# Two bottleneck blocks on one core: a relu moved to ScalarE, the products reordered at the ends of streams, and wider statistics products

## The chip, the cores and the metric

The kernel runs on one core of one Trainium2 chip. The metric is the device time of one execution in microseconds (us). The median of three executions before the change is 1967.26 us, with the others at 1964.27 and 1967.46 us.

The engines are called as the profile calls them: PE is TensorE (matmuls), PEld its weight loads, DVE is VectorE, ACT is ScalarE, POOL is GpSimd, SP is SyncE, which here only issues transfers. A "q" behind an engine's name means its queue: the part that waits and issues transfers.

## The reference

The program computes two bottleneck blocks of a residual network, one after the other, in float32, on 64 images of 1024 channels and 14 x 14 pixels. Cut to what matters, one block is:

```python
out = relu(bn(conv(x, w1, b1)))          # 1x1, 1024 -> 256 channels
out = relu(bn(conv(out, w2, b2, pad=1))) # 3x3,  256 -> 256
out = bn(conv(out, w3, b3))              # 1x1,  256 -> 1024
out = softplus(residual_scale)[0] * out
return relu(x + out)
```

`bn` takes the mean and variance of each channel over all 64 images, so each convolution must be complete (or its statistics known) before its result is normalised. Block 1 has its own weights and takes block 0's output as `x`.

## The kernel before, in words

**Stages.** The 64 images are cut into 32 tiles (T) of two images (PX = 392 pixels). In order of time: the first 1x1 convolution of block 0 (0 to 300 us), the 3x3 convolution of block 0 (300 to 600), its Gram matrix and the statistics of the third convolution (600 to 690), a fused stage that does the last convolution of block 0 and the first of block 1 side by side (690 to 1280), the 3x3 convolution of block 1 (1280 to 1565), its Gram matrix and statistics (1565 to 1660), and the last stage, which does the third convolution of block 1, the residual sum and the final relu (1660 to the end). Block 0's output goes through DRAM (`mid`) and is loaded again in the last stage.

**Seven products for eight.** The 1x1 convolutions are done by a scheme with seven block products instead of eight. Class `Seven` (L253) names them `p1` to `p7`, and each is followed by what takes it out of PSUM (`after1` to `after7`). Three banks are used by a unit: `y` takes p1, and then p6, p7 and p4 are added to it; `x` takes p2; `p` takes p5, and then p3 is added to it. Between the additions, ScalarE copies the bank out (`saved`: u1 after p1, u2 after p6, u3 after p7), because the next product adds to the same bank. So p6 waits for u1, p7 for u2, p4 for u3, and p3 waits until VectorE has added what p5 left in `p` to the residual (`after5`, `add`, L458).

**The stream.** `stream` (L299) puts units one behind the other, so that each unit's last two products, p3 and p4, stand after the next unit's p1. A unit in the middle gives PE the order p1, p3 and p4 of the unit before, p6, p2, p5, p7. All matmuls keep the program's order. `beside` runs a piece of other work between products in the first stage. There are four streams: the first stage, the two of the fused stage, and the last stage.

**The last stage.** `final` (L1134) walks over pairs of tiles. A pair has four units (q = 0 to 3); each `Conv3Pair` (L495) makes channel slots q and q + 4 (rows 0 and 1) of both tiles (i = 0, 1). Its seven products are one matmul of 392 columns each, which the profile shows as two records. Around them stand, for each unit: four adds from PSUM to the residual on VectorE (L458, after2, after5, after3, after4), three copies on ScalarE (L325, `cu`), three adds on GpSimd (L479 for u3, L505 twice for u1 and u2), and four relus with the shift. Row 0's two relus are on ScalarE in `end` (L507), row 1's two on VectorE in `go_out` (L512, the operation at L516), which then sends both rows of both tiles out (L520). Once per pair, `column_sums` (L415, operations at L422 to L425) makes the inputs t1 to t4 of the next pair's products on VectorE. `go_out` of a unit is called when the generator of units is resumed, as are the loads of two further tiles (L123, `x<-mid`, five buffers), which wait until the tiles that lay in their buffers have gone out. SP issues loads and outputs in one order.

**The statistics of the third convolution.** `conv3_stats` (L1076) gets mean and mean square of each output channel from the Gram matrix. It makes `by_mean`, the weights times the mean of their input channel, with two scaled copies on ScalarE (L1092) and an add on GpSimd (L1093); `q`, the weights times a product with the Gram matrix, on VectorE (L1104, L1105); and sums both over the partitions by matmuls whose moving operand is a single column of ones: eight for `by_mean` and eight for `q`, all into one bank `ax`. One copy (L1110) brings them to SBUF, `affine` (L1215) makes scale and shift out of them, and `residual` (L1115) then begins to add the first tile's products, some of which (`made`) PE has done meanwhile.

**The start.** `busy` (L170) gives PE products that nothing uses, of the identity with one of its columns, while the first data are on their way.

## Time and profile before

| what | value |
| --- | --- |
| median of three executions | 1967.26 us |
| profiled execution, its span | 1971.1 us |
| PE busy | 1932.2 us (98%) |
| DVE busy | 1578.6 us (80%) |
| ACT busy | 1022.2 us (52%) |
| POOL busy | 545.0 us (28%) |
| moved between DRAM and SBUF | 408.39 MB, mean 207 GB/s |
| mean granted TensorE clock | 0.994 of full speed |

The span is what one execution took under the profiler. Busy shares are means over stages with different limits, so they don't tell what an edit is worth; the view of windows (busy time of each engine in a given stretch of the span) and the timeline (single instructions with the idle time before them and what ended it) do. The end of a matmul in a trace is modelled; where a number here rests on matmuls, it is taken from their starts.

### The profile page before, as it was taken

Reading aid. Unit: us, or ns where it says so; the run is one execution under the profiler, and the core shown is the slowest. Engines: PE = TensorE matmul, PEld = TensorE weight load, DVE = VectorE, ACT = ScalarE, POOL = GpSimd, SP = SyncE. Lnnn points to the kernel's source line nnn. Section 1 sums busy time; section 2 is a strip of 40 time slices with the busy share of each in tenths; the row PEclk is TensorE's granted clock in tenths of the full one; section 3 lists DMA queues with packets and bytes.
Section 4 is the critical chain, followed back from the end, with each engine's and each line's share of the span. In section 5 each row is a group of like instructions: output and inputs, shape, how many; then the busy total and the mean of one; then the engine's idle time right before and its main releaser. Section 6 shows DMA issues by size and latency. Waiting matters only on the chain.

```text
span 1971.1 us, 27055 instructions
## 1 busy us (share of the span) xinstructions
PE 1932.2 (98%) x9428; PEld 1617.8 (82%) x9428; DVE 1578.6 (80%) x2544; ACT 1022.2 (52%) x2026; POOL 545.0 (28%) x640
## 2 busy tenths in 40 slices
PE   9999999999999999999999999989999999999998
PEld 5555557999998799999999999989999886555555
DVE  5778768999997667677776776699999975889997
ACT  2222214676765155555555555457677632555555
POOL 0111100100105133433433433200010051666665
PEclk9999999999999999999999999999999999999999
DMA  7776725676748534444444444257676395799998
GB/s 289 276 249 247 259 99 167 176 209 196 199 135 211 187 132 187 172 164 180 180 164 176 182 167 168 95 183 210 197 197 200 117 213 217 262 325 334 339 330 296
DMA packets 188983, 408.39 MB, mean 207 GB/s; under 512 B 24944, under 2 KB 165136, under 8 KB 172336
## 3 DMA queue, kind: packets, MB, share of 16 engines
q1 hardware_dynamic: 161728, 324.66, 48.3%
q0 software_dynamic: 21504, 30.94, 6.9%
q10 hardware_dynamic: 5616, 51.06, 6.2%
q8 instruction: 75, 1.23, 0.3%
q14 instruction: 60, 0.49, 0.1%
HBM read 263.75 MB, written 115.34 MB: 192 GB/s over the span
## 4 chain that ended last, share of the span: by engine, by line
PE 85%; DVE 7%; DMA 5%; issue 1%; ACT 1%; SPq 0%; POOL 0%; DVEq 0%; ACTq 0%
PE ay L168 17%; PE cy L168 13%; PE columns L168 13%; PE cp L168 11%; PE ap L168 10%; PE m L168 6%; PE l L168 6%; PE ax L168 5%; PE cx L168 4%; DMA x<-mid 3%; DVE x L458 1%; DMA out<-x 1%; PE ps L168 1%; DVE x L516 1%; DMA home<-y 1%
## 5 line engine op out<-in xcount | busy, mean ns | idle before, releaser
L325 ACT ACTIVATE cu<-cy,scale 128x196 f32<-128x196 f32 (+1 forms) x552 | 256.8, 474 | 299.5 <-PE cy L168 292.2
L168 PE MATMUL columns<-v,ub 128*128 128x224 f32 (+1 forms) x1536 | 303.4, 339 | 0.7 <-ACT columns L755 0.7
L168 PEld LDWEIGHTS columns<-v,ub 128*128 128x128 f32 x1536 | 271.3, 190 | 4.5 <-ACT columns L755 1.2
L325 ACT ACTIVATE x<-x,shift 128x392 f32<-128x392 f32 x368 | 211.5, 614 | 68.6 <-POOL x L484 53.1
L458 DVE SCALAR_TENSOR_TENSOR x<-cp,scale,x 128x196 f32<-128x196 f32 (+1 forms) x368 | 178.0, 484 | 84.8 <-PE cp L168 81.3
L168 PE MATMUL cy<-ct,ws 128*128 128x196 f32 (+1 forms) x736 | 221.8, 383 | 2.5 <-ACT cu L325 2.5
L479 POOL TENSOR_TENSOR x<-x,cu 128x196 f32<-128x196 f32 (+1 forms) x184 | 167.3, 909 | 171.5 <-ACT cu L325 170.8
L168 PE MATMUL ay<-at,ws 128*128 128x196 f32 (+1 forms) x752 | 209.3, 381 | 1.0 <-ACT au L325 1.0
L484 POOL TENSOR_TENSOR x<-x,cu 128x392 f32<-128x392 f32 x124 | 125.9, 1015 | 191.1 <-DVE x L458 181.4
L168 PEld LDWEIGHTS ay<-at,ws 128*128 128x128 f32 x752 | 136.3, 190 | 35.1 <-ACT au L325 1.9
L168 PEld LDWEIGHTS cy<-ct,ws 128*128 128x128 f32 x736 | 133.6, 190 | 36.9 <-ACT cu L325 3.8
L168 PE MATMUL m<-sums,ua 128*128 128x224 f32 (+1 forms) x752 | 147.1, 339 | 6.2 <-DVE sums L619 6.2
L168 PE MATMUL l<-diffs,ub 128*128 128x224 f32 (+1 forms) x768 | 149.7, 338 | 2.5 <-PE columns L168 2.5
L505 POOL TENSOR_TENSOR x<-x,cu 128x392 f32<-128x392 f32 x120 | 125.0, 1042 | 84.2 <-DVE x L458 74.6
L866 POOL DMA_DIRECT2D y<-f x24 | 31.1, 1533 | 414.2 <-DVE f L796 414.2
L168 PEld LDWEIGHTS l<-diffs,ub 128*128 128x128 f32 x768 | 133.8, 189 | 6.6 <-PE columns L168 5.1
L168 PEld LDWEIGHTS m<-sums,ua 128*128 128x128 f32 x752 | 131.6, 190 | 8.4 <-DVE sums L619 8.0
L325 ACT ACTIVATE au<-ay 128x196 f32<-128x196 f32 (+1 forms) x141 | 53.6, 380 | 156.8 <-PE ay L168 156.2
L458 DVE SCALAR_TENSOR_TENSOR x<-cx,scale,x 128x196 f32<-128x196 f32 (+1 forms) x184 | 89.1, 484 | 52.1 <-PE cx L168 51.5
L168 PE MATMUL cx<-y,w 128*128 128x196 f32 (+1 forms) x404 | 126.4, 399 | 0.0
L168 PE MATMUL cy<-y,w 128*128 128x196 f32 (+1 forms) x404 | 125.3, 396 | 0.0
L168 PE MATMUL cp<-zt 128*128 128x257 f32 x392 | 118.9, 385 | 2.0 <-DVE zt L1025 1.7
(209 smaller groups left out, 3997.4 us busy)
## 6 DMA issues: line engine op xcount, KB each, us to landing
x<-in_x SPq DMA_DIRECT2D x62, 1568.0 KB, 6.7
ub<-u SPq DMA_DIRECT2D x94, 768.0 KB, 5.2
x<-mid SPq DMA_DIRECT2D x32, 1568.0 KB, 9.1
mid<-x ACTq DMA_DIRECT2D x31, 1568.0 KB, 5.1
out<-x SPq DMA_DIRECT2D x123, 392.0 KB, 7.0
ua<-u SPq DMA_DIRECT2D x94, 256.0 KB, 3.0
u<-y POOLq DMA_DIRECT2D x48, 256.0 KB, 6.3
home<-y SPq DMA_DIRECT2D x90, 96.0 KB, 4.8
```

What stands on the lines that cost most here:

```text
L168: tc.keep_in_program_order(nc.tensor.matmul(*args, **kw))
L325: tc.keep_in_program_order(nc.scalar.activation(*args, **kw))
L458: nc.vector.scalar_tensor_tensor(v, bank, self.scale[:, o : o + 1], v, ALU.mult, ALU.add)
L479: nc.gpsimd.tensor_add(self.part(1, 1), self.part(1, 1), u3)
L484: nc.gpsimd.tensor_add(v, v, self.u12)
L505: nc.gpsimd.tensor_add(v, v, self.u12[:, i * self.n : (i + 1) * self.n])
L516: nc.vector.tensor_scalar(v, v, self.shift[:, o : o + 1], 0.0, ALU.add, ALU.max)
L866: nc.gpsimd.dma_start(out=out_rows[0][:, o], in_=f[:, o], accum_op=ALU.add)
```

## The change

There are five edits.

1. In `Conv3Pair`, one of row 1's two relus (i = 1) moves from VectorE (`go_out`) to ScalarE (`end`, first of three).
2. `stream` looks one unit ahead. The first unit of a stream does p2 before p6, and the last unit does p2 after p7 instead of before p5, so that a product stands where PE would have waited for a ScalarE copy. To know which unit is the last, the generator is now resumed before a unit's products are issued, where it was resumed after them. What the generator does on being resumed (in the last stage `go_out`, the loads and `column_sums`) is thereby called one unit earlier.
3. In `conv3_stats` the sums over the partitions stream 64 equal columns of ones instead of one, into two banks (`ax`, `ap`) with a copy from each.
4. There too, `by_mean` is made by two VectorE operations instead of two on ScalarE and one on GpSimd.
5. The products at the start use a tile of ones that VectorE sets, instead of the identity, and there are three instead of two.

```diff
     def stream(items, beside=lambda: None):
-        before = None
-        for now in items:
+        before, items = None, iter(items)
+        now = next(items)
+        while now is not None:
+            following = next(items, None)
             yield from now.p1()
             if before is not None:
                 beside()
                 yield from before.last()
                 beside()
+            else:
+                yield from now.p2()
             yield from now.p6()
             if before is not None:
                 before.end()
-            beside()
-            yield from now.p2()
+                if following is not None:
+                    beside()
+                    yield from now.p2()
             beside()
             yield from now.p5()
             beside()
             yield from now.p7()
             beside()
-            before = now
+            if following is None:
+                yield from now.p2()
+            before, now = now, following
         yield from before.last()
         before.end()
...
         def end(self):
-            for i in range(2):
-                o, v = self.o[0], self.part(0, i)
+            for row, i in (1, 1), (0, 0), (0, 1):
+                o, v = self.o[row], self.part(row, i)
                 act(v, v, AF.Relu, bias=self.shift[:, o : o + 1])

         def go_out(self):
-            for i in range(2):
-                o, v = self.o[1], self.part(1, i)
-                tc.keep_in_program_order(
-                    nc.vector.tensor_scalar(v, v, self.shift[:, o : o + 1], 0.0, ALU.add, ALU.max)
-                )
+            o, v = self.o[1], self.part(1, 0)
+            tc.keep_in_program_order(nc.vector.tensor_scalar(v, v, self.shift[:, o : o + 1], 0.0, ALU.add, ALU.max))
...
-        quad = psum.tile(2 * CS, "ax").rearrange("p (o k) -> p o k", k=2)
+        wide = 64
+        sums = [psum.tile(CS * wide, tag).rearrange("p (o k) -> p o k", k=wide) for tag in ("ax", "ap")]
...
-        by_mean, more = (spare[:, s * C : (s + 1) * C] for s in range(MS))
-        for s, to in enumerate((by_mean, more)):
-            nc.scalar.activation(to, w3[:, s].rearrange("p o c -> p (o c)"), AF.Identity, scale=means[s])
-        nc.gpsimd.tensor_add(by_mean, by_mean, more)
+        ones = ones[:, :1].to_broadcast([P, wide])
+        by_mean, w = spare[:, :C], [w3[:, s].rearrange("p o c -> p (o c)") for s in range(MS)]
+        nc.vector.tensor_scalar(by_mean, w[0], means[0], None, ALU.mult)
+        nc.vector.scalar_tensor_tensor(by_mean, w[1], means[1], by_mean, ALU.mult, ALU.add)
...
         for o in range(CS):
-            matmul(quad[:, o, 0:1], by_mean[:, o * P : (o + 1) * P], ones, start=True, stop=True)
+            matmul(sums[0][:, o], by_mean[:, o * P : (o + 1) * P], ones, start=True, stop=True)
         for o in range(CS):
-            matmul(quad[:, o, 1:2], q[:, 0, o * P : (o + 1) * P], ones, start=True, stop=True)
-        nc.vector.tensor_copy(mv, quad)
+            matmul(sums[1][:, o], q[:, 0, o * P : (o + 1) * P], ones, start=True, stop=True)
+        nc.vector.tensor_copy(mv[:, :, 0], sums[0][:, :, 0])
+        nc.vector.tensor_copy(mv[:, :, 1], sums[1][:, :, 0])
...
+    ones = y_all[:, 0, NPX // 2 : NPX // 2 + P]
+    nc.vector.memset(ones, 1.0)
...
-        busy(psum, "ay", 2)
+        busy(psum, "ay", 3, ones)
```

More of the change, by code (lines that the diff above doesn't have):

```diff
@@ L168, in matmul, with busy @@
         tc.keep_in_program_order(nc.tensor.matmul(*args, **kw))
-    def busy(psum, tag, n):
+    def busy(psum, tag, n, with_=None):
+        v = ident if with_ is None else with_
         for i in range(n):
-            matmul(psum.tile(448, tag), ident, ident[:, :1].to_broadcast([P, 448]), start=True, stop=True)
+            matmul(psum.tile(448, tag), v, v[:, :1].to_broadcast([P, 448]), start=True, stop=True)
     def filters(pieces, spare):
```

## The prediction

> **What bounds the kernel now.** I read the page first: busy time and the chain that ended last.

> ```profile
> PE 1932.2 (98%) x9428; PEld 1617.8 (82%) x9428; DVE 1578.6 (80%) x2544; ACT 1022.2 (52%) x2026; POOL 545.0 (28%) x640
> ...
> PE 85%; DVE 7%; DMA 5%; issue 1%; ACT 1%; SPq 0%; POOL 0%; DVEq 0%; ACTq 0%
> ```

> PE is busy nearly throughout and carries 85% of the chain. So a gain can only come from PE's idle pieces and from stretches in which PE is busy but slow. I looked for the slow stretches in the view of windows, cut at the two statistics stages (columns after the colon: length, busy time of PE, PEld, DVE, ACT and POOL, then the granted clock).

> ```profile
> 672.79:676.21 3.42, 3.42 (x25) 2.72 (x23) 2.66 (x4) 0.00 (x0) 0.12 (x1) 1.00 0.00 0
> 676.21:679.62 3.41, 3.41 (x14) 3.02 (x14) 1.03 (x6) 0.10 (x1) 0.00 (x0) 0.50 0.88 283
> 679.62:683.03 3.41, 3.41 (x6) 1.69 (x5) 3.07 (x18) 0.37 (x2) 0.00 (x0) 0.50 0.45 190
> ...
> 1652.42:1655.83 3.41, 3.41 (x11) 2.46 (x11) 2.17 (x9) 0.30 (x1) 0.00 (x0) 0.50 0.91 327
> ```

> In block 0 PE runs at half clock for 6.83 us; in block 1 too (the window 1655.83 to 1659.24 has 0.50 as well). The chain in order of time shows what that does in block 1:

> ```profile
> 1649.64 3.98 PE ax L168 x32
> 1653.62 2.82 PE cx L168 x4
> 1656.44 2.61 PE cy L168 x4
> ...
> 1661.85 1.32 PE cp L168 x4
> ```

> The single-column products (`ax`) lead to the drop, and two of the products behind them take 2.82 and 2.61 us where the same product takes 1.32 at full clock.

> PE's idle pieces at the ends of streams are in the timeline, in brackets with what ended them:

> ```profile
> 30.76 2.90 PE L168 MATMUL ay<-at,ws 128*128 128x392 f32 x8 [0.59 <-ACT au L325]
> ...
> 300.28 2.90 PE L168 MATMUL ay<-at,w 128*128 128x392 f32 x8 [0.65 <-ACT au L325]
> ...
> 1277.44 1.59 PE L168 MATMUL ay<-at,w 128*128 128x196 f32 x8 [0.48 <-ACT au L325]
> ...
> 1667.64 0.93 PE L168 MATMUL cy<-ct,ws 128*128 128x392 f32 x2 [1.19 <-ACT cu L325]
> ```

> The last stage is closer to a tie. The groups of instructions from 1690 to 1945 us, the waits, and three stretches of timeline and chain:

> ```profile
> L516 DVE TENSOR_SCALAR x<-x,shift 128x392 f32<-128x392 f32 x107 | 82.7, 811 | 0.0
> ...
> L325 ACT ACTIVATE x<-x,shift 128x392 f32<-128x392 f32 x106 | 62.0, 613 | 12.8 <-POOL x L505 12.4
> ...
> SPq L123 <- DMA out<-x: 19.0, 23, 2.8
> ...
> 1863.63 0.93 PE L168 MATMUL cp<-y,ws 128*128 128x392 f32 x2 [0.26 <-DVE x L458]
> ...
> 1875.13 0.83 DVE L423 TENSOR_TENSOR ct<-ct,y 128x392 f32<-128x392 f32 x1
> ...
> 1877.54 2.03 DVE L516 TENSOR_SCALAR x<-x,shift 128x392 f32<-128x392 f32 x2
> ...
> 1772.64 6.00 DMA out<-x
> 1778.70 7.52 DMA x<-mid
> ...
> 1787.12 0.93 PE cp L168 x2
> ```

> By the starts of matmuls, 0.329 us apart when nothing waits, a unit takes 14 x 0.329 = 4.61 us and a pair of tiles 18.44. Measured it is 19.07 (p1 at 1690.94 and 1710.01 in the chain). All of the difference is in front of p3, which waits for VectorE's add after p5: at each change of pair, where VectorE also does `column_sums`, two such waits, 0.12 and 0.30 us, each with a first matmul 0.10 slower: 0.62 us a pair. In six pairs the second wait is longer, together by 3.0 us, because a tile came late: the chain there goes output, load, p3. Elsewhere PE doesn't wait.

> [...] L516 takes 0.41 us alone and 0.80 to 1.19 when a GpSimd add is running at its start. Adds from PSUM (L458) stay at 0.61 to 0.63. [...]

> **The change, part by part.**

> *64 columns.* At full clock the first 16 single-column matmuls start 0.106 us apart (673.87 to 675.57). A 129-column matmul of the Gram stage starts 0.11 after the one before. So I price a 64-column one at 0.107, no dearer than now; its array time would be 64/392 x 0.329 = 0.054 us, so at least half of each window is streaming. Is that enough to hold the clock? By columns streamed (0.84 ns each: 0.329 us over 392), the window from 1280.37 streams 45% and keeps full clock, the one from 594.29 streams 37% and loses it. With 64 columns the worst windows stream 57 to 66% (where full products share them). I take it that the clock holds.
> Block 0: the 32 matmuls take 3.41 instead of 4.54 us (1.1), the next product 1.32 instead of 2.75 (1.4), three quarters of the one after at full clock (0.9): 3.5. The fifth product then waits for VectorE's first residual add to free its bank. `affine` needs 3.4 us after the last sum now and a little less with the first copy done ahead, so this add ends near 681.4, and the product starts at 681.5 instead of 684.73. Gain 3.2.
> Block 1: 0.6 + 1.4 + 1.3 + 0.2 = 3.5. Six products are made ahead there, so nothing stands in the way. Gain 3.5.

> *`by_mean` on VectorE.* Two operations of 1024 columns, by L516 and L458 some 0.75 and 1.2 us (estimate), in a stretch where VectorE waits 1.7 us for PE. They end about when the first `q` operation may start, and the GpSimd add that stretched L1105 to 1.24 and 1.53 us is gone. Nothing gained or lost beyond 0.2.

> *Order at ends of streams.* From the starts of matmuls, slower first matmul included: start and end of the first stream 0.85 and 0.91; end of the fused stage 0.75; start of the last stage's stream 0.66 (p2 fills half of the wait, the rest stays, since p6 still waits for u1 behind the relus); start of the fused one 0.33; end of the last 0.33. Sum 3.8. PE sets the pace on both sides of each.

> *Third relu on ScalarE.* ScalarE has three copies of 0.59 and would have three relus of 0.61 in a unit of 4.61: 3.6 us. The relus stand behind u2, and u3 behind them. From the timeline: u2 starts at 1870.52, operations follow each other after 0.51, so u3 could start at 1872.56 instead of 1872.49, and it must be done only by 1873.6, when p4 wants it. The relus wait for GpSimd adds (L479, L505), but the last of these is done at 1875.53 for a relu that now starts near 1876.6. So no new wait for PE in an ordinary unit.
> On VectorE 60 operations of 0.81 go. But in an ordinary unit VectorE holds up nobody, and at the change of pair its order also changes: in the built program the operation for t1 (L424) stands before the add after p5, and no longer behind the relus. From p6's end VectorE then does L423 (0.83[...]), L425 (0.57), the add after p2, L424 (0.55) and only then the add after p5, which ends at about +3.2 us, where p3 wants it at +2.6. One wait of about 0.6 plus 0.1 takes the place of two that sum to 0.62. So this edit brings nothing, and 14 changes of pair may cost 1.3 together.

> *Generator one unit ahead.* Outputs and loads of the last stage are issued a unit, 4.6 us, earlier against PE. A cycle of transfers (two loads, eight outputs) takes about 19.4 us (between the loads issued at 1738.49 and 1932.80 lie ten) against PE's 19.1, so loads drift later by 0.3 a pair. Now that eats the 3 us of slack within some four pairs, and PE waits 3.0 us in all. With 7.7 us of slack it doesn't in 14 pairs. Gain 3.0, net of the line above about 2.

> *Start.* The first useful product would start at about 5.5 instead of 4.52 us behind three cold dummies; but PE waits at 8.18 for data anyway. Cost 0.1.

> Sum: 3.2 + 3.5 + 3.8 + 2.0 - 0.1 = 12.4. From 1967.3 that gives 1955.

> **The rivals.**
> *VectorE's relief counts in full.* If the waits before p3 vanish, 14 x 0.62 = 8.7 more, but then PE at 18.44 a pair runs into the transfers at 19.4 after some eight pairs. About 1949. For it: 0.81 us less per unit on the engine that PE waits for. Against: the new place of L424.
> *The last stage keeps its time.* Transfers may be the true limit (DMA share 0.92 to 0.97 there), or the wait before p3 gets longer. Then 2 to 4 less gain: 1958.
> *The clock drops all the same.* If 64 columns don't count as busy, 6 us of the 6.7 stay: 1961.
> *ScalarE becomes the limit.* If the three relus with their waits for GpSimd delay u3 by 0.3 us in each of 60 units, 18 us are lost: 1973, slower than before. For it: ACT already waits 12.4 us for L505 there. Against: the slack of about 0.4 us above.

> **How the numbers follow.** The forecast gets 0.55, the rivals 0.15, 0.15, 0.08 and 0.07. The time is the forecast's. The range 1948 to 1963 takes in the first three rivals and leaves out the last. Faster by over 0.2% means under 1963.3: 0.86; within 0.2%: 0.07; slower: 0.07.

> **What would show it.** Right: granted clock 1.00 right after the `ax` and `ap` products, and 1.32 us for each product behind them; no idle before the second product of a first unit; in the last stage one wait of 0.6 to 0.7 us a pair before p3, VectorE's group of relus halved with PE's pair still at 19.1, and no load ended by a tile's first add. Wrong: a clock of 0.50 there; waits of p4 or p7 for ACT; pairs at 18.5 or above 19.3.

## The result and the profile after

The median went from 1966.68 us (seven executions) to 1959.24 us (seven executions, 1958.05 to 1959.69): a ratio of 0.9964, with a 95% interval of 0.9953 to 0.9976. That is 7.4 us or 0.38% less. The forecast was 1955, from a sum of 12.4.

The page of the changed kernel, its busy times and its chain:

```profile
PE 1919.9 (98%) x9430; PEld 1614.4 (82%) x9430; DVE 1552.4 (79%) x2491; ACT 1041.5 (53%) x2082; POOL 532.0 (27%) x638
...
PE 90%; DVE 7%; issue 1%; ACT 1%; DMA 1%; SPq 0%; POOL 0%; DVEq 0%
```

PE lost 12.3 us of busy time (1932.2 before) and carries 90% of the chain instead of 85%; the share of DMA in it fell from 5% to 1%. The windows at the two statistics stages (columns as before: length, busy PE, PEld, DVE, ACT, POOL, granted clock, DMA share, GB/s):

```profile
673.52:676.94 3.42, 3.42 (x25) 2.94 (x25) 1.65 (x10) 0.30 (x1) 0.00 (x0) 1.00 0.60 183
676.94:680.35 3.41, 3.41 (x11) 1.82 (x10) 3.31 (x17) 0.82 (x2) 0.00 (x0) 1.00 0.69 289
1642.91:1646.32 3.41, 3.41 (x26) 3.02 (x26) 1.64 (x7) 0.06 (x1) 0.00 (x0) 1.00 0.49 136
1646.32:1649.74 3.42, 3.42 (x12) 2.00 (x11) 3.32 (x18) 0.24 (x1) 0.00 (x0) 1.00 0.81 336
```

The clock is 1.00 in all four, where before it was 0.50 for 6.83 us in each block. The chain in block 1 shows the products behind the sums at full speed:

```profile
1641.95 1.73 PE ax L168 x16
1643.68 1.79 PE ap L168 x16
1645.47 1.37 PE cx L168 x4
1646.84 1.32 PE cy L168 x4
```

At the start of the first stream, the timeline of PE has no wait in brackets any more, since p2 (`ax`) stands between p1 and p6:

```profile
27.20 2.80 PE L168 MATMUL ay<-x,w 128*128 128x392 f32 x8
29.83 2.80 PE L168 MATMUL ax<-x,w 128*128 128x392 f32 x8
32.46 1.81 PE L168 MATMUL ay<-at,ws 128*128 128x392 f32 x5
```

In the last stage one wait a pair remains. First the waits of the stretch 1690 to 1925 us (total, times, longest), then the timeline of VectorE at one change of pair:

```profile
PE cp L168 <- DVE x L466: 5.6, 13, 0.4
```

```profile
1843.20 0.83 DVE L431 TENSOR_TENSOR ct<-ct,y 128x392 f32<-128x392 f32 x1
1844.07 0.57 DVE L433 TENSOR_TENSOR ct<-y,ct 128x392 f32<-128x392 f32 x1
1844.55 0.62 DVE L466 SCALAR_TENSOR_TENSOR x<-cx,scale,x 128x392 f32<-128x392 f32 x1
1845.09 0.56 DVE L432 TENSOR_TENSOR ct<-y 128x392 f32<-128x392 f32 x1
1845.56 0.62 DVE L466 SCALAR_TENSOR_TENSOR x<-cp,scale,x 128x392 f32<-128x392 f32 x1
1846.10 0.64 DVE L522 TENSOR_SCALAR x<-x,shift 128x392 f32<-128x392 f32 x1
```

The line at 1845.09 is t1's operation; behind it, at 1845.56, starts the add after p5 that p3 waits for. In the kernel before, t1's operation (L424) came behind that add and the relus:

```profile
1877.01 0.62 DVE L458 SCALAR_TENSOR_TENSOR x<-cp,scale,x 128x392 f32<-128x392 f32 x1
1877.54 2.03 DVE L516 TENSOR_SCALAR x<-x,shift 128x392 f32<-128x392 f32 x2
1879.49 0.55 DVE L424 TENSOR_TENSOR ct<-y 128x392 f32<-128x392 f32 x1
```

By the starts of matmuls p3 now comes 0.60 us late, with 0.10 more in its second matmul, in every pair, and a pair takes 19.13 us (p3 at 1846.23 and 1865.37). No load is late.

Between the two profiled executions the gain is 13.7 us (spans of 1971.1 and 1957.5), which is close to the sum. Between ordinary executions it is about half of that. The profiled execution of the kernel before took 1972.9 us of device time, 5.7 more than the median from which the forecast was counted down; 12.4 off its own time would have been 1960.5. So the question for the experiments is what the profiled execution of the kernel before had that its other executions don't have, and what each edit is worth by itself. Theory A says that the drop of the clock depends on where the clock's window falls (a stretch of 3.41 us: up to the last product the low stretches of both profiles last 3.41 or 6.83 us). Rival B says that every execution pays it, and another part of the forecast is missing.

### The profile page after: what moved, and what is told of

It reads as the page before. It is cut to its first block, busy times and chain, and to the rows that moved or that the text cites. A ratio compares the mean times of both kernels' runs of the same rounds, so it can differ in the third digit from the quotient of the medians.

```text
span 1957.5 us, 26989 instructions
## 1 busy us (share of the span) xinstructions
PE 1919.9 (98%) x9430; PEld 1614.4 (82%) x9430; DVE 1552.4 (79%) x2491; ACT 1041.5 (53%) x2082; POOL 532.0 (27%) x638
## 4 chain that ended last, share of the span: by engine, by line
PE 90%; DVE 7%; issue 1%; ACT 1%; DMA 1%; SPq 0%; POOL 0%; DVEq 0%
PE ay L168 17%; PE cy L168 16%; PE columns L168 13%; PE cp L168 12%; PE ap L168 10%; PE m L168 6%; PE l L168 6%; PE ax L168 4%; PE cx L168 4%; PE ps L168 1%; DVE x L466 1%; DVE ct L431 1%; DVE f L801 0%; DMA home<-y 0%; DVE ct L433 0%
## 5 line engine op out<-in xcount | busy, mean ns | idle before, releaser
L168 PE MATMUL columns<-v,ub 128*128 128x224 f32 (+1 forms) x1536 | 301.1, 337 | 0.7 <-ACT columns L760 0.7
L168 PEld LDWEIGHTS columns<-v,ub 128*128 128x128 f32 x1536 | 269.4, 188 | 4.1 <-ACT columns L760 1.2
L333 ACT ACTIVATE x<-x,shift 128x392 f32<-128x392 f32 x428 | 239.7, 613 | 55.1 <-POOL x L492 53.2
L168 PE MATMUL cy<-ct,ws 128*128 128x196 f32 (+1 forms) x736 | 222.0, 383 | 1.1 <-ACT cu L333 1.1
L168 PE MATMUL ay<-at,ws 128*128 128x196 f32 (+1 forms) x752 | 209.2, 381 | 0.0
L487 POOL TENSOR_TENSOR x<-x,cu 128x196 f32<-128x196 f32 (+1 forms) x184 | 159.2, 865 | 174.1 <-ACT cu L333 162.5
L168 PEld LDWEIGHTS ay<-at,ws 128*128 128x128 f32 x752 | 136.4, 190 | 33.6 <-ACT au L333 0.5
L168 PEld LDWEIGHTS cy<-ct,ws 128*128 128x128 f32 x736 | 133.4, 190 | 36.4 <-ACT cu L333 3.8
L168 PE MATMUL m<-sums,ua 128*128 128x224 f32 (+1 forms) x752 | 147.6, 340 | 6.2 <-DVE sums L624 6.2
L168 PE MATMUL l<-diffs,ub 128*128 128x224 f32 (+1 forms) x768 | 149.7, 338 | 3.0 <-PE columns L168 2.9
L168 PEld LDWEIGHTS l<-diffs,ub 128*128 128x128 f32 x768 | 133.6, 189 | 7.0 <-PE columns L168 5.9
L168 PEld LDWEIGHTS m<-sums,ua 128*128 128x128 f32 x752 | 132.2, 191 | 8.7 <-DVE sums L624 7.9
L168 PE MATMUL cx<-y,w 128*128 128x196 f32 (+1 forms) x404 | 124.1, 392 | 0.4 <-DVE x L1130 0.4
L168 PE MATMUL cy<-y,w 128*128 128x196 f32 (+1 forms) x404 | 123.8, 392 | 0.0
L168 PE MATMUL cp<-zt 128*128 128x257 f32 x392 | 118.8, 385 | 1.8 <-DVE zt L1030 1.7
```

The costliest lines, as they stand in the source:

```text
L168: tc.keep_in_program_order(nc.tensor.matmul(*args, **kw))
L333: tc.keep_in_program_order(nc.scalar.activation(*args, **kw))
L487: nc.gpsimd.tensor_add(self.part(1, 1), self.part(1, 1), u3)
```

## Experiments

### The kernel before again, and the 64 columns alone

`e0_before` is the kernel before without an edit.

> The kernel before, unchanged, so that many of its executions can be set side by side with their mean clocks. Theory A [...]: the executions spread over some 3 us or more, from about 1963 to 1969, and the longer ones have the lower mean clock; one low window of 3.41 us is 0.0009 of mean clock and costs 1.7 us. A second profile of it need not show 6.83 us of half clock at both statistics stages, and its span then is 2 to 5 us shorter than 1971.1. Theory B (both drops are paid in full every time, and another predicted gain is absent in ordinary executions): the executions lie within 1 us of each other, the clock doesn't vary with the time, and the second profile shows 6.83 us of half clock at both stages again.

Measured: 13 executions from 1963.85 to 1968.95, median 1966.3, ratio 1.0 (0.9992 to 1.0008). Together with the other executions of the kernel before that ran beside the experiments up to the one before the last there are 116: median 1966.16, from 1962.97 to 1970.33, with a mean clock of 0.996 on average. Only three of the 116 have a clock of 0.994 or less, and these took about 1970. The execution that the prediction was read from had 0.994 and, at 1972.9, was longer than all of them. Between 0.995 and 0.997 time and clock hardly order (medians of 1966.3, 1966.4 and 1965.5). The new profile, in windows that begin where its clock windows do:

```profile
673.21:676.62 3.41, 3.41 (x33) 3.38 (x31) 1.61 (x3) 0.00 (x0) 0.00 (x0) 1.00 0.27 52
676.62:680.03 3.41, 3.41 (x8) 2.04 (x8) 2.89 (x19) 0.30 (x1) 0.00 (x0) 0.50 0.89 357
680.03:683.44 3.41, 3.41 (x12) 1.91 (x11) 2.71 (x7) 1.82 (x4) 0.00 (x0) 1.00 0.18 70
1646.01:1649.42 3.41, 3.41 (x23) 2.52 (x21) 3.23 (x4) 0.00 (x0) 0.79 (x1) 1.00 0.02 5
1649.42:1652.84 3.42, 3.42 (x22) 2.73 (x22) 1.71 (x7) 0.30 (x1) 0.00 (x0) 1.00 0.75 246
```

In block 0 the single-column products fall into one window, and one low window follows in place of two. In block 1 they are split over two windows, and none is low. It is the same program; only the windows lie elsewhere. The low ones of the first profile all begin a whole number of times 3.413 us behind its first one (348.53 us; 597.70 is 73 times, 676.21 is 96, 1324.74 is 286, 1652.42 is 382). In `e0_before` the windows at the sums of both blocks begin 0.4 us later (673.21 against 672.79 and 1649.42 against 1649.01), and the first single-column product starts 0.5 and 2.0 us earlier (673.40 against 673.87 and 1647.63 against 1649.64). That the windows lie elsewhere holds outside the statistics stages too: up to the last product, the first profile has seven low windows (at 348.5, 597.7, 676.2, 679.6, 1324.7, 1652.4 and 1655.8 us), this one four (348.9, 676.6, 1321.7 and 1570.9) and the changed kernel's two (345.8 and 595.0). At some 1.7 us each (half of 3.41), five windows are 8.5 of the 13.7 us by which the first profile is longer than the changed kernel's. The way from the first single-column product to the first p6 behind these products took 17.98 and 18.16 us in the first profile and 16.32 and 14.80 in this one: 5.0 us less with no edit. Theory A stands, as far as this goes.

`e1_wide` is the kernel before with the width alone (with the second bank and the second copy that belong to it):

```diff
-        quad = psum.tile(2 * CS, "ax").rearrange("p (o k) -> p o k", k=2)
+        wide = 64
+        sums = [psum.tile(CS * wide, tag).rearrange("p (o k) -> p o k", k=wide) for tag in ("ax", "ap")]
...
+        ones = ones[:, :1].to_broadcast([P, wide])
...
```

> The kernel before with the 64 equal columns, two banks and two copies alone. The prediction's working: 3.2 and 3.5 us less in an execution that would have paid both drops in full; no low window at the statistics stages. Theory A: in the median 3 to 5 us below the kernel before, and less spread. Theory B: 6 to 7 us below. If the width has no part in it: 0 to 0.5 us.

Measured: 1963.57 (1961.8 to 1964.95, 21 executions), ratio 0.9987 (0.9981 to 0.9994): 2.5 us, not 6.7, and somewhat less than theory A's 3 to 5. No window at the statistics stages is low, and the same two ways take 14.72 and 14.80 us. The mean clock rises from 0.9960 to 0.9971; a low window is worth 0.0009, so on average some 1.3 windows vanish, each worth about 1.7 us. That is 2.2 and close to the 2.5.

### Width taken back in the changed kernel

`e7_narrow`:

```diff
-        wide = 64
+        wide = 1
```

> The changed kernel with a single column again in the statistics' products (two banks and two copies kept). Theory A (the cost depends on where the clock window falls): median 2 to 3.5 us above the changed kernel, a spread of 3 us or more, mean clock mostly 0.996 to 0.997 in place of 0.998, the longer executions with the lower clock. Theory B: every execution 6 to 7 us longer. If the width has no part: the changed kernel's time.

Measured: 1963.62 (1960.52 to 1965.51, 21 executions), ratio 0.9986 (0.9980 to 0.9993). That is 4.4 us above the changed kernel, more than theory A's 2 to 3.5 and less than B's 6 to 7. The spread is 5 us where the changed kernel's is 1.6, and the times order with the clock: medians of 1964.64 at 0.996, 1963.40 at 0.997 and 1960.78 at 0.998. The dependence on the clock is as A says; the mean size depends on the kernel around it. The profile of `e7_narrow` has one low window in each block; the two ways take 16.46 and 16.62 us, where the changed kernel's take 14.70 and 14.80, together 3.6 us more. Since the second bank and copy are still there, it is the width that keeps the clock (1.00 at both stages of the changed kernel). Why the single column costs more here than in the kernel before stays open.

### The relu alone

`e2_relu` is the kernel before with the third relu on ScalarE:

```diff
-            for i in range(2):
-                o, v = self.o[0], self.part(0, i)
+            for row, i in (1, 1), (0, 0), (0, 1):
+                o, v = self.o[row], self.part(row, i)
...
```

> The kernel before with the third relu on ScalarE alone. Predicted: nothing, or up to 1.3 us longer (one wait of about 0.7 us per change of pair before p3, with t1's operation standing before the add after p5). Rival, VectorE's relief counts: up to 8.7 us less. Rival, ScalarE becomes the limit: 6 us or more longer, with u3 ending after p4 wants it.

Measured: 1959.79 (1958.86 to 1962.01, seven executions), ratio 0.9973 (0.9962 to 0.9983): 6.3 us less by the medians, 5.3 by the ratio. The prediction had 0 or a loss. VectorE's timeline at a change of pair:

```profile
1845.57 0.62 DVE L458 SCALAR_TENSOR_TENSOR x<-cx,scale,x 128x392 f32<-128x392 f32 x1
1846.11 0.62 DVE L458 SCALAR_TENSOR_TENSOR x<-cp,scale,x 128x392 f32<-128x392 f32 x1
1846.64 0.93 DVE L514 TENSOR_SCALAR x<-x,shift 128x392 f32<-128x392 f32 x1
1847.49 1.37 DVE L424 TENSOR_TENSOR ct<-y 128x392 f32<-128x392 f32 x1
```

Here t1's operation (L424) stands behind the relu, and the add after p5 comes before both. The waits before p3 are 0.12 + 0.10 and 0.04 + 0.10 us a pair, and a pair takes 18.80 us in place of 19.07. Only one wait is longer, by 0.1 us. From block 1's first statistics product to the last product of the kernel lie 306.45 us, against 310.82 in `e0_before` (neither has a low window there), and 0.45 less behind it: 4.8 us by the traces. Of this the waits give 13 x 0.26 = 3.4, and late loads, 0.55 in `e0_before`, are gone. So the relu by itself does bring something, and it doesn't move t1's operation. Since the changed kernel has that operation in front of the add, another edit must put it there: theory C names the generator. Rival D says that the generator is a gain by itself, and that it and the relu get rid of the same late loads.

### The edit to the stream, and the generator one unit ahead alone

`e3_stream` is the kernel before with edit 2 as it stands in the diff of the change. `e4_look` has only the generator ahead:

```diff
-        before = None
-        for now in items:
+        before, items = None, iter(items)
+        now = next(items)
+        while now is not None:
+            following = next(items, None)
...
-            before = now
+            before, now = now, following
```

> The kernel before with the edit to the stream alone (order at the ends, generator a unit ahead). Predicted: 3.8 from the order and 3.0 from the loads that are no longer late, together 6.8 us less, some 4 of it if the late loads are of the profiled execution only. The waits before p3 stay as in the kernel before (0.12 and 0.30 a pair, each with 0.10 in the next matmul).

> The kernel before with the generator one unit ahead, the order of products unchanged. Theory C (being ahead puts t1's operation in front of the add after p5, whichever engine does the relu): one wait before p3 of 0.60 + 0.10 us a pair in place of 0.12 + 0.10 and 0.30 + 0.10, so 0.08 x 13 = 1.0 us longer from that, and no late load, 0.8 to 3.0 us shorter from that: 1964 to 1966 us. Rival D (being ahead is a gain by itself, as the prediction had it): 3 us below the kernel before, 1963.

Measured: `e3_stream` 1961.58 (15 executions), ratio 0.9979 (0.9971 to 0.9986), 4.5 us less; `e4_look` 1966.49 (13 executions), ratio 0.9999 (0.9990 to 1.0007). Being ahead brings nothing. VectorE's timeline of `e4_look` at a change of pair, with both of row 1's relus still on VectorE:

```profile
1849.32 0.62 DVE L459 SCALAR_TENSOR_TENSOR x<-cx,scale,x 128x392 f32<-128x392 f32 x1
1849.86 0.56 DVE L425 TENSOR_TENSOR ct<-y 128x392 f32<-128x392 f32 x1
1850.33 0.62 DVE L459 SCALAR_TENSOR_TENSOR x<-cp,scale,x 128x392 f32<-128x392 f32 x1
1850.87 1.74 DVE L517 TENSOR_SCALAR x<-x,shift 128x392 f32<-128x392 f32 x2
```

This is the order of the changed kernel: t1's operation (L425) in front of the add after p5, and a wait of 0.60 + 0.10 in every pair. `e3_stream` has the same. So it is the generator, not the relu, that moves the operation. `e3_stream` did worse than the 6.8 written for it and close to the "some 4" that was written for the case that late loads belong to the profiled execution only; its wait before p3, 0.70 a pair instead of the unchanged 0.62, costs 1.0 of it. Its executions with a clock of 0.997 or 0.998 have a median of 1960.1, those with 0.996 or less one of 1964.0.

### The changed kernel with one part undone

`e5_nolook` keeps the changed order of products, but is told the number of units instead of asking for the next one:

```diff
-    def stream(items, beside=lambda: None):
+    def stream(items, beside=lambda: None, units=0):
...
-            following = next(items, None)
+            final_unit = k == units - 1
```

> The changed kernel with its order of products, but with the generator not ahead (the number of units is given instead). Theory C: the waits before p3 are those of the kernel with the relu alone, 0.12 + 0.10 and 0.04 + 0.10, in place of 0.60 + 0.10: 13 x 0.34 = 4.4 us below the changed kernel, about 1954.8. Rival D (the relu and the generator ahead both only get rid of the same late loads, so that either one is enough): the same time as the changed kernel, 1959, or longer by a late load or two.

`e6_reluback` puts both relus of row 1 back on VectorE:

```diff
-            for row, i in (1, 1), (0, 0), (0, 1):
-                o, v = self.o[row], self.part(row, i)
+            for i in range(2):
+                o, v = self.o[0], self.part(0, i)
...
```

> The changed kernel with both of row 1's relus on VectorE again. Theory C: with the generator ahead the relu has no part in the wait before p3, which stays at 0.60 + 0.10 a pair: within 1 us of the changed kernel. If the relu gains by itself in the changed kernel too: 4 to 6 us longer.

Measured: `e5_nolook` 1954.95 (1954.13 to 1957.14), ratio 0.9941 (0.9929 to 0.9954); `e6_reluback` 1959.93 (1958.97 to 1960.89), ratio 0.9966 (0.9954 to 0.9978). Theory C named 1954.8 and the changed kernel's time within 1 us. In `e5_nolook` the waits are 0.12 + 0.10 and 0.04 + 0.10 again, 0.34 less than 0.70 in each of 13 pairs, or 4.4 us. In `e6_reluback` they are 0.60 + 0.10, as in the changed kernel. Without the generator ahead the changed kernel would have gained 11.3 us.

`e10_rest` undoes edits 4 and 5 in the changed kernel:

```diff
-        nc.vector.tensor_scalar(by_mean, w[0], means[0], None, ALU.mult)
-        nc.vector.scalar_tensor_tensor(by_mean, w[1], means[1], by_mean, ALU.mult, ALU.add)
+        for s, to in enumerate((by_mean, more)):
+            nc.scalar.activation(to, w3[:, s].rearrange("p o c -> p (o c)"), AF.Identity, scale=means[s])
+        nc.gpsimd.tensor_add(by_mean, by_mean, more)
...
-        busy(psum, "ay", 3, ones)
+        busy(psum, "ay", 2)
```

> The changed kernel with by_mean made by ScalarE and GpSimd again and the start as before (identity, two products). Predicted: by_mean on VectorE is worth 0 +- 0.2, the start costs 0.1: the changed kernel's time within 0.5 us. Rival (the new by_mean or the new start is a hidden loss or gain): more than 1 us away from it.

Measured: 1959.07, ratio 0.9962 (0.9948 to 0.9976). The two edits together are worth nothing that can be measured.

### Taking the rest of the wait away

`e8_spread` is `e5_nolook` with two buffers for each of `column_sums`' tiles and its operations given out over the units of the pair before:

```diff
+    def column_steps(pool, ys, n):
+        v = [pool.tile([P, n], FP, tag=f"ct{i}", name=f"ct{i}", bufs=2) for i in range(4)]
...
+        yield nc.vector.tensor_sub(t3, ys[1][1], ys[0][1])
...
                     yield units[-1]
+                    next(now[2], None)
...
```

> The kernel of the run before last (changed kernel, generator not ahead), in which all four of column_sums' tiles have two buffers, and its four operations are given out one per unit of the pair before instead of all at the change of pair. Theory C in full (only VectorE's order at the change of pair keeps PE waiting): no wait before p3, the pair at 18.44 instead of 18.80, 13 x 0.36 = 4.7 us less, about 1950. If the transfers set the pace below 18.8 us a pair: loads come late and the time stays at 1953 to 1955. [...]

Measured: 1969.87 (21 executions), ratio 1.0017 (1.0010 to 1.0023): worse than every other one. It was no test of spreading, as VectorE's timeline shows:

```profile
1911.10 0.63 DVE L473 SCALAR_TENSOR_TENSOR x<-cp,scale,x 128x392 f32<-128x392 f32 x1
1911.64 1.01 DVE L440 TENSOR_TENSOR ct<-y 128x392 f32<-128x392 f32 x1
1912.58 1.38 DVE L438 TENSOR_TENSOR ct<-y 128x392 f32<-128x392 f32 x1
1913.88 0.41 DVE L529 TENSOR_SCALAR x<-x,shift 128x392 f32<-128x392 f32 x1
1914.21 0.55 DVE L439 TENSOR_TENSOR ct<-ct,y 128x392 f32<-128x392 f32 x1
1914.68 0.61 DVE L473 SCALAR_TENSOR_TENSOR x<-cp,scale,x 128x392 f32<-128x392 f32 x1
```

Where nothing fixes their place, three of the four operations came together at the end of the pair, the fourth two adds later, and p3 waits 1.45 + 0.10 us there. In `e9_pinned` each is kept in the program's order:

```diff
-        yield nc.vector.tensor_sub(t3, ys[1][1], ys[0][1])
+        yield tc.keep_in_program_order(nc.vector.tensor_sub(t3, ys[1][1], ys[0][1]))
...
```

> As the run with column_sums given out over the units, but its four operations keep their place in the program's order, so that each stands behind a unit's add after p5 and in front of that unit's relu (in the earlier one all four came together between two adds). Theory C in full: no wait before p3, the pair at 18.44 us, 13 x 0.36 = 4.7 us below the changed kernel without the generator ahead: about 1950. If the transfers set the pace: loads come late, 1953 to 1955. If the longer VectorE sequence (four adds of 0.62, a relu and an operation of 0.6 to 1.4) delays an add after p5 in every unit: 1955 or more.

Measured: 1954.54, ratio 0.9940 (0.9926 to 0.9954), the time of `e5_nolook`, and what was written for the case that the transfers set the pace. From 1690 to 1825 us no product waits and the pair takes 18.44 us; then p3 comes late by 0.5 to 1.1 us in each pair. The waits of the stretch, and one of them in the timeline:

```profile
DVE x L473 <- DMA x<-mid: 3.9, 4, 1.5
...
PE cp L168 <- DVE x L473: 3.9, 6, 0.9
```

```profile
1845.36 0.63 DVE L473 SCALAR_TENSOR_TENSOR x<-cp,scale,x 128x392 f32<-128x392 f32 x1 [0.98 <-DMA x<-mid]
```

The first add on a tile waits for its load. The loads issued at 1839.2 and 1916.5 are four pairs apart: 19.3 us a pair against PE's 18.44. So the transfers take over from VectorE, some nine pairs into the stage. A reason to have the generator ahead after all is that it issues outputs and loads a unit earlier. `e11_both` is the changed kernel itself, generator ahead, with the fixed and spread operations.

> The changed kernel itself (generator one unit ahead), with column_sums' operations in the program's order, one per unit, and two buffers for each of its tiles. Theory C in full: with the operations kept behind the add after p5, being ahead no longer costs the 0.70 us a pair, and transfers begin a unit (4.6 us) earlier, so that loads that fall behind by about 0.9 a pair (19.3 against 18.44) come late only in the last one or two pairs in place of the last six: 13 x 0.70 = 9.1 us below the changed kernel, less 0 to 2 for late loads: 1950 to 1952. If being ahead doesn't move the transfers forward: as the run without it, 1954.5. If the order puts a wait back before p3: 1957 or more.

Measured: 1949.51 (1948.83 to 1950.97, five executions), ratio 0.9918 (0.9905 to 0.9932): 9.7 us below the changed kernel (8.7, if each is compared with the kernel before that ran beside it), and the shortest of all. VectorE's timeline, and the group of p3 in the stretch from 1690 to 1925 us (busy, mean ns, then idle before):

```profile
1846.71 0.63 DVE L475 SCALAR_TENSOR_TENSOR x<-cx,scale,x 128x392 f32<-128x392 f32 x1 [0.25 <-PE cx L168]
1847.37 0.63 DVE L475 SCALAR_TENSOR_TENSOR x<-cp,scale,x 128x392 f32<-128x392 f32 x1
1847.91 1.01 DVE L442 TENSOR_TENSOR ct<-y 128x392 f32<-128x392 f32 x1
1848.85 1.17 DVE L531 TENSOR_SCALAR x<-x,shift 128x392 f32<-128x392 f32 x1
```

```profile
L168 PE MATMUL cp<-y,ws 128*128 128x392 f32 x102 | 42.0, 493 | 0.0
```

The operation (L442) now stands behind the add after p5, one in each unit, and VectorE waits for PE rather than PE for VectorE. One matmul in the stretch starts late, by 0.02 us (and 0.10 in the next).

## Why the prediction came out as it did

The direction and the range were right, but the range of 15 us was wide; the forecast had 5 us too much gain, and the rival "The last stage keeps its time" with its 1958 came closer than the forecast's 1955. By its own steps:

*64 columns.* The mechanism was right: the clock stays at 1.00, the products behind take 1.32 to 1.37 us, and the first 16 of the 64-column products start 0.108 us apart on the mean (673.50 to 675.23 in `e1_wide`; 0.107 was taken). The term was mis-sized: 6.7 is what the profiled execution had to lose, and 2.5 (`e1_wide`) is what the median had (4.4, by `e7_narrow`, in the changed kernel). The cost differs from run to run: 6.83 us of half clock in both blocks in one execution, 3.41 and none in the next, where the windows lie elsewhere. The prediction took one execution's windows for every execution's. There was a sign of it beforehand: the profiled span was 1971.1 us, and even that was above the median of 1967.26. Gains read in a long execution were taken off the median of shorter ones.

*`by_mean` and the start.* Right: nothing that can be measured together (`e10_rest`). The two operations took 0.75 and 1.28 us, where 0.75 and 1.2 were estimated. The first product is at 5.12 us in place of 4.52 (the 448-column matmuls ahead of it start 0.75 us apart in the kernel before, from 2.28 to 4.52, where 448 times 0.84 ns would be 0.38), but the first p1 of the stream at 27.20 against 27.38 (27.44 in `e10_rest`).

*Order at ends of streams.* About right in its sum: 3.8 was predicted, as 1.8, 1.1 and 1.0 for the three stages. From traces with and without it, the first stage's stream is 1.5 us shorter (277.80 against 279.34 from its first p1 to the next stage), the fused stage 1.5 (603.54 in the changed kernel against 605.07 in `e1_wide`, from the statistics' first product), the last stage 0.4 (`e3_stream` against `e4_look`): together 3.4.

*Relu.* Right in its result and wrong in its reason. In the changed kernel the relu is worth 0.7 us by medians of executions whose ranges overlap (`e6_reluback`), and nothing in the traces: from block 1's first statistics product to the end both take 315.69 us. The wait before p3 is the 0.6 + 0.1 a pair that was predicted. That the result came out was luck, though: the step that failed says that with the relu gone VectorE's order at the change of pair changes, so that t1's operation comes before the add after p5. `e4_look` has that order with the relus where they were, and `e2_relu` hasn't got it. The relu alone was worth 6.3; the generator being ahead took most of that back (4.3 between `e5_nolook` and the changed kernel).

*Generator one unit ahead.* Wrong: 3.0 predicted, nothing measured (`e4_look`). No load is late any more, as predicted, but what failed is the size and a cost that the step did not have. The late loads, 3.0 us in the profiled execution, were 0.55 in `e0_before`'s profile and 1.46 in `e1_wide`'s by the same count (each wait above 0.30, summed), and the longer wait costs 13 x 0.08 = 1.0.

Together: 2.5 + 3.4 + 0.7 + 0 = 6.6, where 7.4 was measured with an interval of 4.7 to 9.2. The parts come from different kernels; with the 4.4 of `e7_narrow` for the width the sum would be 8.5. Of the 5.0 that the forecast had too much, the clock is 4.2 by `e1_wide` or 2.3 by `e7_narrow`, and the net of 2.0 for generator and relu, which came out at 0.7 or less, another 1.3. The mean clock also rises from `e1_wide` (0.9971) to the changed kernel (0.998), by about one more low window; which edit does that, the runs don't show.

*The rival "VectorE's relief counts in full"* was held off by t1's place, as the prediction argued against it, but for the wrong edit. What it said would follow came true in `e9_pinned`: PE at 18.44 a pair runs into the transfers, after some nine pairs where eight were reckoned. *"The last stage keeps its time"* came true: a pair takes 19.13 us against 19.07, and from block 1's first statistics product to the end lie 315.7 us against 316.2 in `e0_before`. The reason was its second one, the longer wait before p3 (0.70 against 0.62), and not the transfers, since `e5_nolook` takes 18.80 a pair. *"The clock drops all the same"* fell: no window at the statistics stages is low in any profile with 64 columns. *ScalarE as the limit* fell: no wait of PE for ScalarE in the ordinary units of the last stage.

## What to carry to other kernels

A stall that hangs on where the clock's window falls (here two low windows in each block in one execution, one and none in the next) is worth its mean over executions: compare the time of the profiled execution (here 1972.9 us) with the median (1967.3) before pricing what a trace shows, and take a second profile of the same kernel if they differ. When several edits reach the same engine, ask of each alone what it does to the order of that engine's instructions; here the relu was worth 6.3 us alone and at most 0.7 beside the generator running ahead, because that placed an operation in front of the add that PE waits for. Once such an operation is fixed behind the add that others wait for, a generator that runs ahead turns from a loss (4.3 us, `e5_nolook` against the changed kernel) into the slack that the transfers need (a gain of 5.0, `e11_both` against `e9_pinned`).

## What the runs showed of the hardware

Where PE does not hold them back, the transfers of the last stage bring a pair's two loads and eight outputs, 6.42 MB, in about 19.1 us (`e11_both`, loads issued at 1795.49 and 1909.92, six pairs apart) to 19.3 us (`e9_pinned`), or some 335 GB/s; the windows view gives 340 GB/s for `e11_both` over the stretch 1690 to 1925 us and 337 for `e9_pinned` over 1820 to 1925.

VectorE's relu took 1.17 us in `e11_both` and 0.41 in the line of `e8_spread` shown above, for the same 392 elements, and in `e11_both` it delayed nothing. GpSimd's add was running at the start of the first and not at that of the second, and the first ended 0.23 us after the add did. In the kernel before, from 1690 to 1945 us, all 26 relus that started beside no GpSimd add took 0.41 us, and of the 80 that started during one, 76 took 0.80 to 1.19 and four 0.42 to 0.50. The operation for t2 (L423) started during one in all of its 13 times there and took 0.83; those for t1, t3 and t4 (L424, L422, L425), of 392 elements too, started beside none and took 0.55 to 0.57. VectorE's adds from PSUM (L458) took 0.61 to 0.63 whether one was running at their start or not. In `e11_both` such a relu costs nothing, since what PE needs stands in front of it.
